# Four graph-attention layers in one kernel: who orders the instructions of layers 1 to 3

## The chip, the cores and the metric

The kernel runs on one core of a Trainium2 chip. The metric is the device time of one execution in microseconds (us). A core has five engines that work side by side, each through its own queue in order: TensorE (PE: matrix products; PEld is its weight load), VectorE (DVE), ScalarE (ACT), GpSimd (POOL) and SyncE (SP, which issues transfers). Transfers run on 16 DMA engines. TensorE reads from SBUF and writes its products to PSUM[...].

## What is computed

The input is `x` (4096 rows of 256 numbers) and an adjacency matrix `adj` (4096 x 4096, int32), which has many more edges among the first nodes than among the last. Four attention layers follow each other. Each is added to its input and normalised:

```python
x = _layernorm(x + L0(x, positions, curv_feats, adj, ...))   # 8 heads, with a curvature term
x = _layernorm(x + L1(x, adj, ...))                          # 1 head
x = _layernorm(x + L2(x, adj, ...))                          # 4 heads, elu, residual, its own layer norm
x = _layernorm(x + L3(x, adj, ...))                          # three attention passes, elu after each
```

One pass of layer 3 stands for the kind of work:

```python
Wh = h @ W
e = jax.nn.leaky_relu(Wh @ a[:F] + (Wh @ a[F:]).T, ALPHA)
att = jax.nn.softmax(jnp.where(adj > 0, e, NEG_INF), axis=1)
h = jax.nn.elu(att @ Wh)
```

Layer 1's scores depend on the source node alone within a row's softmax, so its weights are the mask itself times a factor of the source node. Layer 2 does the same as layer 3 for four heads of 64 columns.

## The kernel before

Layer 0 runs first, takes 1379 us of the profiled execution, and writes lists of the nodes that matter to each group of rows. The change doesn't touch it. Layers 1, 2 and 3 (three passes) have one frame, `attend` (L1240).

**Tiles.** The 4096 rows are cut into 16 pairs of row tiles (2 x 128 = 256 rows, `PW`). For one pair, the sum over the source nodes runs over tiles of 128 nodes. The first pairs take all 32 tiles ("dense": 6 pairs in layer 1, 1 in layer 2, 3 in layer 3) and read the values from SBUF (`Vp` or `V`). For the other pairs only listed nodes count, 13 to 25 tiles a pair, and their rows are gathered by GpSimd into `g` (L1284, 1010 gathers in all). `sequence` mixes both kinds into one list of (pair, tile).

**One step of the list.** `weights` makes the weights `w` of a tile from the mask (loaded by SP, L1278):
- layer 1: a cast of the mask, on ACT and DVE in turn (L1382), and for listed tiles a split of `g` in two parts, on ACT (L1359) and then DVE (L1360);
- layer 2: four instructions on DVE, one a head (L1474);
- layer 3: one instruction on DVE (L1567).

`products` multiplies the weights of earlier steps: layer 1 into `acc` (L1393), layer 3 into `acc` (L1573), two row tiles each. Layer 2 takes two tiles at a time (`batch=2`): first the eight products `num` (L1483, 64 columns each, heads in turn in the lower and upper half of the columns), then the eight products `den` (L1487, one column each, four places). A matrix product of this type stands as two records in the trace, in layer 1 as one.

**The ending of a pair.** When a pair's last tile is multiplied, the generator `one` divides, normalises and projects its two row tiles for the next layer. Its instructions hop between engines. In layer 3, for each row tile: `inverse` on DVE (L316 to L318), `y` on ACT (L1583), `y` on DVE (L1585), `elu_neg` twice on ACT (L307, L308), `y` on DVE (L310); then either transposes on TensorE (`xT_p`, L196), copies on ACT (L198) and the projection `ph` (L207), or, in the third pass, the residual (L1589), moments (L301, L302) and the layer norm (L333 to L339). In layer 2, `num` and `den` are copied to `sb` on ACT (L1497, L1498), transposed on TensorE into `pt` (L1505), divided (L316 to L318, L1510), and go through elu and two layer norms before the transposes of `xT_p`.

**The order.** `attend` walks the list and takes a few steps of the ending after each tile (`rate` steps, one `yield` each). So the ending of an earlier pair is interleaved with the weights and products of later ones. This interleaving is written into the source, and `tc.manual_schedule` holds PE, DVE and ACT to the order of the source:

```python
with tc.manual_schedule(engines={mybir.EngineType.PE, mybir.EngineType.DVE, mybir.EngineType.Activation}):
    ...
    for q, k, A, listed in seq:
        if k == 0:
            states[q] = opened(q, A, listed)
        ready.append((states[q], k, weights(states[q], k), k == A - 1))
        if len(ready) == lag + batch:
            multiply(batch)
        due += rate
        while due >= 1.0:
            due -= 1.0
            next(end, None)
```

Outside such a block, the tile scheduler orders the instructions when the kernel is built. It runs through the program with its own estimate of each instruction's duration, and gives an engine that comes free the earliest instruction of the source that it takes to be ready. SP and POOL are ordered so in the whole kernel, and so is everything outside `attend`.

**Buffers.** There are six buffers for `w` in each layer (a buffer of layer 2 holds four heads), six for the masks (four tiles each), 16 for `g` in layers 1 and 2 and 20 in layer 3. In PSUM, six `acc` serve three pairs; layer 2 has three `num` and three `den`. Two more banks serve all other products.

**The seams.** A layer starts when the last row of its projection is there: sums (L229 to L237), extremes (`spread_p`, `spread_q`, L252 to L260), in layers 2 and 3 a row factor that is written to memory and read back as `R` (L290 and on), and the scaling of `V`.

Of the kernel before, what the change touches and what calls it, by code (L numbers as in the profile page):

```python
# [78 lines left out]
def gnn_stack(ctx: ExitStack, tc: tile.TileContext, a: dict, out: bass.AP):  # L79
# [37 lines left out]
    def drain(steps):  # L117
        for _ in steps:
            pass
# [1120 lines left out]
    def attend(seq, opened, weights, products, ends, rate=1.0, batch=1, lag=2):  # L1240

        states, ready, ended, due = {}, [], [], 0.0
        end = ends(ended)
        with tc.manual_schedule(engines={mybir.EngineType.PE, mybir.EngineType.DVE, mybir.EngineType.Activation}):
            def multiply(n):
                some, ready[:] = ready[:n], ready[n:]
                products(some)
                ended.extend(state for state, _, _, last in some if last)  # L1250
# [11 lines that stand above are left out]
            while ready:  # L1262
                multiply(min(batch, len(ready)))
            drain(end)
# [78 lines left out]
    def layer1(proj, nxt, seq):  # L1343
        with ExitStack() as st:
# [51 lines left out]
            def one(state, n):  # L1396
# [14 lines left out]
                yield from project(nxt, ys, q * PW)  # L1411

            attend(seq, opened, weights, products, lambda ended: ends_of(ended, NP, nxt, ps, one))
            nxt.sums()

# [5 lines left out]
    def layer2(proj, V, nxt, seq):  # L1421
# [3 lines left out]
        with ExitStack() as st:  # L1425
# [64 lines left out]
            def one(state, n):  # L1490
# [35 lines left out]
                yield from project(nxt, ys, q * PW)  # L1526

            attend(seq, opened, weights, products, lambda ended: ends_of(ended, NP, nxt, ps, one), rate=1.6, batch=2)
            nxt.sums()

    def layer3(n, proj, V, nxt, seq):
        s = 1.0 - 0.01
        with ExitStack() as st:
# [41 lines left out]
            def one(state, m):  # L1575
# [18 lines left out]
                else:  # L1594
                    yield from project(nxt, ys, q * PW)

            attend(seq, opened, weights, products, lambda ended: ends_of(ended, NP, nxt, ps, one))
            if nxt is not None:
                nxt.sums()
# [110 lines left out]
```

## Time and profile before

| | |
|---|---|
| median of 3 runs | 3496.66 us (3496.36 to 3497.55) |
| the profiled execution's own time | 3482.08 us |
| its span | 3480.4 us |
| TensorE busy | 2684.1 us, 77% of the span |
| VectorE busy | 2300.2 us, 66% |
| GpSimd busy | 1941.0 us, 56% |
| ScalarE busy | 1349.4 us, 39% |
| mean granted TensorE clock | 0.824 |

The median and the profiled execution are different executions, 14.6 us apart. All durations of single instructions come from the profiled one. A line of the groups of instructions names source line, engine, operation, output and inputs, and count; "idle before" is time in which the engine stood still until the named instruction, on its own or another engine, let it go on. Matmuls are pipelined and their ends are modelled, so consecutive records overlap; what one costs in a row of them is read from the distance between starts. A busy share is a mean over stages that have different limits, so the span is cut into stages below.

### The profile page before, as it was taken

Reading aid. Unit: us, or ns where it says so; the run is one execution under the profiler, and the core shown is the slowest. Engines: PE = TensorE matmul, PEld = TensorE weight load, DVE = VectorE, ACT = ScalarE, POOL = GpSimd, SP = SyncE. Lnnn points to the kernel's source line nnn. Section 1 sums busy time; section 2 is a strip of 40 time slices with the busy share of each in tenths; the row PEclk is TensorE's granted clock in tenths of the full one; section 3 lists DMA queues with packets and bytes.
Section 4 is the critical chain, followed back from the end, with each engine's and each line's share of the span. In section 5 each row is a group of like instructions: output and inputs, shape, how many; then the busy total and the mean of one; then the engine's idle time right before and its main releaser. Section 6 shows DMA issues by size and latency. Waiting matters only on the chain. (4 is left out here: it accounts for less than half of the span.)

```text
span 3480.4 us, 53129 instructions
## 1 busy us (share of the span) xinstructions
PE 2684.1 (77%) x15814; PEld 1998.9 (57%) x15814; DVE 2300.2 (66%) x7414; ACT 1349.4 (39%) x3868; POOL 1941.0 (56%) x1874
## 2 busy tenths in 40 slices
PE   6475567767778766888688787777699989989885
PEld 5354455555556554777544333333488868867674
DVE  7798877786555443555488888778455545545665
ACT  3354446554445443455431222233312222232333
POOL 0264555666777761455158655553177637746772
PEclk8576656667787666988899999999799989989998
DMA  6587777664444443555343333332444454436552
GB/s 183 160 263 247 223 224 234 192 204 117 119 121 115 122 112 113 172 147 144 99 125 101 100 99 100 97 90 57 130 135 137 118 156 135 136 95 185 154 154 81
DMA packets 345903, 495.62 MB, mean 142 GB/s; under 512 B 120444, under 2 KB 252386, under 8 KB 345602
## 3 DMA queue, kind: packets, MB, share of 16 engines
q0 software_dynamic: 87600, 252.16, 25.9%
q1 hardware_dynamic: 239576, 223.18, 21.6%
q10 hardware_dynamic: 18432, 16.79, 1.4%
q8 instruction: 131, 2.15, 0.3%
q14 instruction: 164, 1.34, 0.1%
HBM read 426.20 MB, written 65.72 MB: 141 GB/s over the span
## 5 line engine op out<-in xcount | busy, mean ns | idle before, releaser
L1284 POOL DMA_INDIRECT g<-table,pair_idx x1010 | 1111.5, 1101 | 597.9 <-PE den L1487 95.8
L648 POOL DMA_INDIRECT g<-table,idx x445 | 502.1, 1128 | 285.2 <-issue 151.3
L1573 PE MATMUL acc<-g,w 128*128 128x257 f32 x2448 | 576.7, 384 | 36.3 <-DVE w L1567 36.3
L1573 PEld LDWEIGHTS acc<-g,w 128*128 128x128 f32 x2448 | 461.1, 191 | 112.6 <-DVE w L1567 49.0
L1474 DVE SCALAR_TENSOR_TENSOR w<-R,g,mask 128x256 f32<-128x256 f32 x1004 | 425.4, 493 | 23.0 <-PE den L1487 18.5
L1483 PE MATMUL num<-w,g 128*64 128x256 f32 x2008 | 319.5, 422 | 51.6 <-DVE w L1474 50.9
L1567 DVE SCALAR_TENSOR_TENSOR w<-R,g,mask 128x256 f32<-128x256 f32 x612 | 282.1, 480 | 100.4 <-PE acc L1573 98.0
L1003 POOL DMA_INDIRECT pair_m<-in_adjT,cell x251 | 269.7, 1075 | 136.7 <-issue 46.0
L692 PE MATMUL acc<-g,to_row 128*128 128x264 f32 x890 | 325.9, 528 | 18.3 <-DVE g L679 16.2
L1573 PE MATMUL acc<-V,w 128*128 128x257 f32 x1152 | 288.3, 390 | 22.4 <-DMA R<-r_d 17.5
L692 PEld LDWEIGHTS acc<-g,to_row 128*128 128x128 f32 x890 | 225.9, 268 | 77.6 <-DVE g L679 20.5
L1483 PEld LDWEIGHTS num<-w,g 128*64 128x64 f32 x2008 | 157.5, 148 | 196.1 <-DVE w L1474 135.0
L1573 PEld LDWEIGHTS acc<-V,w 128*128 128x128 f32 x1152 | 221.4, 195 | 60.2 <-ACT V L1553 18.1
L1583 ACT ACTIVATE y<-acc,inverse 128x256 f32<-128x256 f32 x96 | 45.6, 475 | 516.2 <-DVE inverse L318 444.2
L207 PE MATMUL ph<-wx,xT 128*128 128x258 f32 (+3 forms) x640 | 204.4, 456 | 34.7 <-ACT xT L198 30.0
L628 PE MATMUL x<-what,of_row 128*128 128x40 f32 (+4 forms) x890 | 157.1, 350 | 55.9 <-DVE of_row L625 54.3
L891 DVE FIND_INDEX8 cand<-ones,near 128x8 uint16<-128x520 bf16 (+8 forms) x424 | 195.0, 469 | 0.0
L628 PEld LDWEIGHTS x<-what,of_row 128*128 128x128 f32 x890 | 153.2, 265 | 66.4 <-DVE of_row L625 54.9
L686 ACT ACTIVATE to_row<-count,side 128x128 f32<-128x128 f32 x445 | 145.3, 391 | 115.1 <-PE acc L692 111.4
L1007 DVE TENSOR_SCALAR pair_mb<-pair_m 128x256 uint8<-128x256 int32 x251 | 74.8, 300 | 172.0 <-DMA pair_m<-in_adjT,cell 153.5
L1567 DVE SCALAR_TENSOR_TENSOR w<-R,V,mask 128x256 f32<-128x256 f32 x288 | 135.3, 480 | 69.9 <-PE acc L1573 55.1
L207 PEld LDWEIGHTS ph<-wx,xT 128*128 128x128 f32 x640 | 137.0, 224 | 73.9 <-ACT xT L198 44.8
(325 smaller groups left out, 4608.1 us busy)
## 6 DMA issues: line engine op xcount, KB each, us to landing
ai<-in_adj SPq DMA_DIRECT2D x124, 512.0 KB
mask<-listed_d SPq DMA_DIRECT2D x228, 128.0 KB
at<-in_adjT SPq DMA_DIRECT2D x96, 256.0 KB
mask<-mask_d SPq DMA_DIRECT2D x128, 128.0 KB
g<-table,pair_idx POOLq DMA_INDIRECT x1010
R<-r_d SPq DMA_DIRECT2D x56, 256.0 KB
table<-V POOLq DMA_DIRECT2D x12, 1032.0 KB
s<-y ACTq DMA_DIRECT2D x96, 128.0 KB
```

The lines of the kernel that those rows point to most:

```text
L207: nc.tensor.matmul(ph, xT[:, kt, :], self.wx[:, kt, :], start=kt == 0, stop=kt == 1 and self.bias is None)
L628: nc.tensor.matmul(self.x[:, t], of_row[:, t], ls.what, start=True, stop=True)
L648: nc.gpsimd.indirect_dma_start(self.g[:, t, :], None, table0[:, :], bass.IndirectOffsetOnAxis(ap=self.idx[:, t:t + 1], axis=0))
L686: nc.scalar.activation(self.to_row[:, t], count, AF.Abs, bias=self.side[:, t, 0:1])
L692: nc.tensor.matmul(acc, self.to_row[:, t], self.g[:, t, 0:VW], start=self.t0 + t == 0, stop=last and t == n - 1)
L891: nc.vector.max_index(cand[:, s], ones8, near[:, at:at + W])
L1003: nc.gpsimd.indirect_dma_start(m[:, :], None, pair_cells, bass.IndirectOffsetOnAxis(ap=cell[:, k:k + 1], axis=0))
L1284: nc.gpsimd.indirect_dma_start(g[:, :], None, self.table[:, :], bass.IndirectOffsetOnAxis(ap=pair_idx[:, at:at + 1], axis=0))
L1474: nc.vector.scalar_tensor_tensor(w[:, h], R[:, h].rearrange("p t i -> p (t i)"), g[:, VW2 + h:VW2 + h + 1], m, ALU.max, ALU.mult)
L1483: nc.tensor.matmul(num[h % 2 * D2:(h % 2 + 1) * D2, h // 2, :], g[:, h * (D2 + 1):h * (D2 + 1) + D2], w[:, h], start=False, stop=last and ...
L1567: nc.vector.scalar_tensor_tensor(w, R[:, q * PW:(q + 1) * PW], g[:, C + 1:C + 2], m, ALU.max, ALU.mult)
L1573: nc.tensor.matmul(t, w[:, it * P:(it + 1) * P], g[:, 0:C + 1], start=k == 0, stop=last)
```

## The change

In `attend`, the block that holds PE, DVE and ACT to the order of the source becomes an ordinary block. These engines are then ordered by the tile scheduler in layers 1 to 3 too. The source still sets the order in which the scheduler prefers instructions. Nothing else in the source differs.

```diff
         states, ready, ended, due = {}, [], [], 0.0
         end = ends(ended)
-        with tc.manual_schedule(engines={mybir.EngineType.PE, mybir.EngineType.DVE, mybir.EngineType.Activation}):
+        if True:
             def multiply(n):
                 some, ready[:] = ready[:n], ready[n:]
                 products(some)
```

## The prediction

> **What bounds the kernel now.** I read the page's engine shares first (TensorE 77%, VectorE 66%, no engine full), so the answer differs by stage. I then cut the span where the lines of a layer begin and end, and asked for busy times per stretch. Columns: stretch, length, busy us (instructions) of PE, PEld, DVE, ACT and POOL, granted TensorE clock, DMA share, GB/s.
>
> ```profile
> 1420.00:1699.00 279.00, 240.36 (x1470) 216.32 (x1469) 155.72 (x532) 145.03 (x499) 139.17 (x143) 0.89 0.49 140
> 1699.00:1741.00 42.00, 17.23 (x57) 11.52 (x55) 13.74 (x56) 16.69 (x65) 1.41 (x2) 0.73 0.31 96
> 1741.00:2453.00 712.00, 565.00 (x4844) 266.64 (x4844) 589.05 (x1557) 204.07 (x617) 392.17 (x285) 0.91 0.34 94
> 2453.00:2488.00 35.00, 7.71 (x29) 4.78 (x25) 11.40 (x48) 18.92 (x52) 0.96 (x1) 0.64 0.26 77
> 2488.00:2783.00 295.00, 294.24 (x1376) 255.94 (x1376) 170.76 (x448) 73.85 (x274) 204.71 (x207) 0.99 0.51 143
> 2783.00:2811.00 28.00, 11.28 (x32) 6.94 (x32) 7.96 (x37) 14.77 (x52) 0.94 (x1) 0.63 0.25 78
> 3136.00:3456.00 320.00, 276.43 (x1193) 227.08 (x1192) 198.69 (x552) 98.14 (x166) 202.96 (x206) 0.97 0.54 151
> ```
>
> In order: layer 1, the seam to layer 2, layer 2, its seam, layer 3's first pass and its seam, layer 3's third pass. The second pass and its seam (2811 to 3136) look like the first. Layer 0, 1379 us, is not touched. The first pass is TensorE's, with 0.8 us idle of 295. The third has 183 fewer instructions and takes 25 us longer. In layer 2 neither TensorE nor VectorE is full: VectorE, the busier, stands idle 123 us.
>
> The waits say why. Columns: waiting instruction, what ended the wait, us in total, times, longest. The first three lines are layer 2, the others layer 3's third pass.
>
> ```profile
> PE xT_p L196 <- ACT y L339: 84.1, 15, 6.5
> ...
> PE num L1483 <- DVE w L1474: 50.9, 50, 3.1
> DVE inverse L316 <- PE pt L1505: 50.6, 14, 7.1
> ...
> PE acc L1573 <- DVE w L1567: 41.2, 24, 2.5
> ...
> DVE inverse L316 <- PE acc L1573: 33.9, 14, 2.6
> DVE y L310 <- ACT elu_neg L308: 33.8, 29, 2.2
> ```
>
> These are blocked queues: an instruction of a row tile's ending stands at the head and waits, with ready products or weights behind it. In the third pass VectorE waits 67.7 us on `acc` and `elu_neg`, then TensorE lacks `w` for 41.2 us.
>
> The last view is TensorE's timeline in layer 2. Columns: start, time until the last ends, instruction; a product of one head is two records.
>
> ```profile
> 2049.72 1.95 PE L1483 MATMUL num<-w,g 128*64 128x256 f32 x16
> 2051.59 1.04 PE L1487 MATMUL den<-w,g 128*1 128x256 f32 x16
> 2052.57 0.55 PE L1505 MATMUL pt<-ident,sb 128*128 128x128 f32 x3
> ...
> 2450.53 1.04 PE L1487 MATMUL den<-w,g 128*1 128x256 f32 x16
> 2451.51 1.08 PE L1483 MATMUL num<-w,g 128*64 128x256 f32 x8
> 2452.52 0.61 PE L1487 MATMUL den<-w,g 128*1 128x256 f32 x8
> ```
>
> From start to the next start, 8 `num` cost 1.87 us, 4 `num` 1.01, 8 `den` 0.98. So two `num` (different heads) take (1.87 - 1.01) / 2 = 0.43 us together and each run of `num` 1.87 - 4 x 0.43 = 0.15 more. A run of `den`, with four heads sharing 0.43 us, costs 0.98 - 2 x 0.43 = 0.12 more. **The order of products is a cost of its own here.**
>
> **What the Trainium skill says.** "TensorEngine Tiling (Array Packing)", Key Properties: different tiles of the array run in parallel, and "Changing tiling mode (not just tile) drains the TensorE". The trace agrees: 64-column `num` pair, one-column `den` go in fours, and a change costs 0.12 to 0.15 us. "TensorE: Matmul & The Clock Gate", Architectural detail: ScalarE and VectorE are strict FIFO; Part 2 says that matmuls stay in program order. The waits above are what that means. The same page, Part 1: idle TensorE is throttled. Here the clock is 0.63 to 0.73 in the seams and 0.99 in the first pass.
>
> **The change part by part.** No instruction, transfer or buffer size is added or removed: only the `with` goes, so the tile scheduler puts the instructions of PE, DVE and ACT where its own times say that they are ready. I compared the instruction orders of both programs; the counts are from there. The order of SP's and POOL's issues shifts by places too, but POOL is busy 392 of 712 us in layer 2 and its gathers have 16 buffers and more; I cost that at nothing. If the cover went, 251 gathers in layer 2 late by 0.3 us each would be 75 us.
>
> *Layer 3's third pass.* Before, VectorE meets `inverse` 2 weights after a tile's last one; after, 5 (six buffers hold them). The two row tiles of a pair run their endings side by side with weights between, so the 2.2 us wait for `elu_neg` (a table load on ACT) has four weights in front. At most 7 instructions stand between two weights, some 2.8 us (six of 0.43, one of 0.18), against 5 weights x 0.86 us of products (four records at 294.24 / 1376 = 0.214 us) = 4.3 us in stock. TensorE at the first pass's rate needs 1193 x 0.214 = 255 us instead of 320: 65 at most. VectorE's own work is 199, but some waits will stay; I take **-45** (-20 to -65).
>
> *First and second pass.* TensorE is full, and the order of its products and transposes is the same before and after: **0**. The cover is TensorE itself; if a transpose is late by 1 us per row tile, 64 us are lost, my upper end.
>
> *Layer 1.* TensorE idles 279 - 240 = 39 us, on the weights, `Vg` and transposes; the transposes now stand 45 to 66 products after the tile's end instead of 26 to 64. I take three quarters, **-30** (-10 to -50, the lower end with some clock won).
>
> *Seams.* In the source's order the last row tiles end one after the other. At 1699 two pairs take 14 and 13 us in turn; after, they overlap: -12. Layer 2's seam has one pair, two tiles: -4. The first and second pass end with two pairs of 10 us in turn: -8 each. The tail from 3456 to 3480 is the same chain: -10. Together **-42** (-20 to -55). What comes next at each seam, the projection's sums and the load of `R`, is not shortened.
>
> *Layer 2.* VectorE is unblocked: its waits for `pt` (50.6), `den` (18.5) and `elu_neg` (16.2) can go, and 589 us of work stays. But where TensorE was short of `w`, the scheduler took `den` of a head as soon as its `num` was in. The runs go from 142 + 142 (141 of 8 each) to 487 of `num` (227 of one) and 452 of `den` (259 of one). Pairs of `num` go from 566 to 696, fours of `den` from 283 to 517. Price before: 566 x 0.43 + 142 x 0.15 + 283 x 0.43 + 142 x 0.12 = 404 us. After: 696 x 0.43 + 487 x 0.15 + 517 x 0.43 + 452 x 0.12 = 649. Transposes and projections take some 55 us more (16 pairs x 3.4). So TensorE needs 459 before and **704 after**, over VectorE's 589 and about the 712 that the stage takes now. The 84.1 us wait for `y` before the transposes goes (they stand some 33 heads behind the `pt` instead of 24), but TensorE is now the bound: **0** (-50 if a lone head overlaps its neighbour somewhat, +60 if waits for `w` add to the full TensorE).
>
> Sum: -45 + 0 - 30 - 42 + 0 = -117. The profiled execution took 3482.08 us (span 3480.4 and 1.7 around it), so 3365; the median is 14.6 us above it, so **3380** on its scale.
>
> **The rivals.**
> *A, as above*: 0.55, 3380.
> *B, layer 2 gains too*: VectorE's bound, 589 us plus some waits, holds because lone `num` and `den` overlap. For it: before, VectorE was the busier. Against it: no `num` overlaps a `den` in the trace. Layer 2 at 642 would give 3380 - 70 = 3310. 0.15.
> *C, new waits for old*: the scheduler's times differ from the chip's, half of the 117 comes, and layer 2 loses 40: 3497 - 58 + 40 = 3479. For it: an order fixed by wrong times blocks the same FIFO queues. Against it: in layer 3 the counts above leave slack. 0.15.
> *D, slower*: the hand-over between `num` and `den` is dearer for a lone head than in long runs[...]. TensorE then runs layer 2 well over 704. It decides when the 117 us are lost there: over 939 runs, 0.125 us more each, that is 0.25 to 0.28 instead of 0.12 to 0.15. At 0.2 more, +188 - 117 gives 3568. For it: single runs never occur before, so the price is carried over from runs of 4 and 8. Against it: every change of mode in the trace costs about the same. 0.12, and 0.03 for a result within 0.2%.
> That the change does nothing is out: the orders differ on all three engines.
>
> **How the numbers follow.** The likeliest, A, gives 3380. The range takes A's bounds, most of B and of C: 3300 to 3480. Faster by over 0.2% (about what a measurement of this kernel can tell from no change, 7 us): A, B and C, 0.85. Same 0.03, slower 0.12.
>
> **What would show it.** Layer 3's third pass at about 275 us with TensorE over 90% busy and the waits for `w` nearly gone; passes one and two still 295 to 297; each seam shorter by 8 to 12 us; in layer 2 short runs of `num` and `den` in turn, a lone head costing 0.43 + 0.15 + 0.43 + 0.12 = 1.13 us, TensorE the busier engine, and VectorE waiting for `den`. Layer 2 under 660 makes B right. Layer 2 over 800, with over 0.25 us lost at each change, makes D right. A first pass over 310, or a third pass still over 305, means that the new order blocks too.

## The result, and the profile after

The changed kernel takes 3335.27 us (median of 4 runs, 3333.80 to 3349.82) beside 3497.11 us of the kernel before (4 runs): a ratio of 0.9546 with a 95% interval of 0.9519 to 0.9573, 162 us less. The profiled execution has a span of 3332.1 us and a mean granted clock of 0.855 (0.824 before).

First, the same cut by stage as in the prediction. This is the table of busy times per stretch of the kernel after; columns: stretch, length, busy us (instructions) of PE, PEld, DVE, ACT and POOL, granted TensorE clock, DMA share, GB/s.

```profile
1430.00:1633.00 203.00, 201.26 (x1448) 189.61 (x1447) 143.51 (x529) 146.43 (x500) 144.20 (x145) 1.00 0.68 193
1633.00:1665.00 32.00, 19.76 (x72) 13.33 (x70) 12.91 (x60) 16.70 (x67) 1.41 (x2) 0.78 0.42 129
1665.00:2369.00 704.00, 703.55 (x4820) 249.85 (x4824) 566.60 (x1553) 200.76 (x616) 389.57 (x285) 1.00 0.34 95
2400.00:2694.00 294.00, 292.89 (x1367) 255.05 (x1368) 174.73 (x449) 71.98 (x275) 206.09 (x207) 0.99 0.51 143
2694.00:2713.00 19.00, 9.26 (x43) 6.11 (x41) 7.30 (x35) 13.42 (x51) 0.94 (x1) 0.89 0.36 108
3027.00:3317.00 290.00, 271.08 (x1200) 224.66 (x1200) 190.93 (x558) 94.80 (x172) 204.31 (x207) 1.00 0.59 169
```

In order: layer 1 without its first part, the seam to layer 2, layer 2, layer 3's first pass and its seam, layer 3's third pass. Layer 1 now keeps TensorE busy throughout at full clock (before: 240 of 279 us at 0.89). In layer 2 TensorE is busy in 703.55 of 704 us. Layer 2's clock, 0.91 before, is 1.00. The seams are shorter and run at a higher clock, and the third pass still leaves TensorE 19 us without work.

The exact lengths, from the first to the last attention product of each layer in the two traces (a seam is the time between two of them, the tail the time behind the last; the predicted column repeats the steps of the prediction):

| stage | before, us | after, us | difference | predicted |
|---|---|---|---|---|
| up to layer 1's first product | 1378.8 | 1391.3 | +12.5 | 0 |
| layer 1 | 321.1 | 242.0 | -79.1 | -30 |
| seam to layer 2 | 42.0 | 32.1 | -9.9 | -12 |
| layer 2 | 711.2 | 704.0 | -7.2 | 0 |
| seam to layer 3 | 35.4 | 31.2 | -4.2 | -4 |
| layer 3, first pass | 294.2 | 293.9 | -0.3 | 0 |
| seam | 28.1 | 18.4 | -9.7 | -8 |
| second pass | 293.5 | 294.6 | +1.1 | 0 |
| seam | 28.2 | 19.3 | -8.9 | -8 |
| third pass | 321.1 | 289.8 | -31.3 | -45 |
| tail | 26.6 | 15.4 | -11.2 | -10 |

The rows add up to -148, the difference of the two spans. The first row is no effect of an order that changed: layer 0 is the same, and over the traces of comparable runs its length lies anywhere from 1379 to 1405 us. Without it the stages bring 161 us. The third pass is at its shortest in this trace: in five other comparable traces with the same layer 3 it takes 292.7 to 293.6 us, so its gain is 28 to 31 us.

Second, what VectorE and TensorE wait for after the change. Columns: waiting instruction, what ended the wait, us in total, times, longest. The first three lines are layer 2 (VectorE, then TensorE), the last three the third pass.

```profile
DVE inverse L316 <- PE pt L1505: 73.1, 19, 8.8
DVE w L1474 <- PE den L1487: 52.3, 36, 3.2
...
PE num L1483 <- ACT V L1455: 2.5, 1, 2.5
...
DVE w L1567 <- DMA g<-table,pair_idx: 58.4, 73, 2.4
DVE w L1567 <- PE acc L1573: 35.8, 83, 1.2
...
PE acc L1573 <- DVE w L1567: 18.4, 22, 1.4
```

In layer 2 the direction has turned round: before, TensorE waited 84.1 us for `y` and 50.9 us for `w`; now VectorE waits for `pt` and `den`, and TensorE for 2.5 us. In the third pass the waits for `inverse` and `elu_neg` (33.9 and 33.8 us before) are gone from the top. In their place VectorE waits 58.4 us for the gathers `g`, which it had not waited for in the lines of before.

Third, TensorE's timeline in layer 2 after the change. Columns: start, time until the last ends, instruction, records (two a head).

```profile
1694.46 0.65 PE L1483 MATMUL num<-w,V 128*64 128x256 f32 x4
1695.04 0.59 PE L1487 MATMUL den<-w,V 128*1 128x256 f32 x2
1695.57 0.65 PE L1483 MATMUL num<-w,V 128*64 128x256 f32 x4
1696.15 0.60 PE L1487 MATMUL den<-w,V 128*1 128x256 f32 x6
```

These are the short runs. Two heads of `num` cost 0.58 us from start to next start (0.43 + 0.15 in the prediction), one head of `den` 0.53 (0.43 + 0.12).

### The profile page after: what moved, and what is told of

Same layout as the page of the kernel before. It is cut to its first block, busy times and chain, and to the rows that moved or that the text cites. A ratio compares the mean times of both kernels' runs of the same rounds, so it can differ in the third digit from the quotient of the medians.

```text
span 3332.1 us, 53082 instructions
## 1 busy us (share of the span) xinstructions
PE 2771.2 (83%) x15814; PEld 1953.9 (59%) x15814; DVE 2262.0 (68%) x7414; ACT 1333.9 (40%) x3866; POOL 1947.7 (58%) x1874
## 4 chain that ended last, share of the span: by engine, by line
PE 48%; DMA 4%; DVE 3%; ACT 2%; issue 1%; POOL 0%; SPq 0%; ACTq 0%; DVEq 0%; POOLq 0%
PE acc L1573 19%; PE num L1483 11%; PE den L1487 8%; PE acc L1393 4%; PE ph L207 4%; DMA g<-table,pair_idx 3%; PE xT_p L196 1%; PE pr L213 1%; DVE w L1567 1%; PE pt L1505 0%; POOL g L1284 0%; ACT V L1553 0%; DMA V<-V_d 0%; DMA table<-V 0%; DVE y L1585 0%
## 5 line engine op out<-in xcount | busy, mean ns | idle before, releaser
L1474 DVE SCALAR_TENSOR_TENSOR w<-R,g,mask 128x256 f32<-128x256 f32 x1004 | 440.9, 491 | 48.0 <-PE den L1487 47.9
L1567 DVE SCALAR_TENSOR_TENSOR w<-R,g,mask 128x256 f32<-128x256 f32 x612 | 292.0, 482 | 244.2 <-PE acc L1573 165.0
L1483 PE MATMUL num<-w,g 128*64 128x256 f32 x2008 | 367.6, 395 | 0.0
L1003 POOL DMA_INDIRECT pair_m<-in_adjT,cell x251 | 276.8, 1103 | 133.3 <-issue 44.2
L692 PE MATMUL acc<-g,to_row 128*128 128x264 f32 x890 | 326.6, 529 | 20.5 <-DVE g L679 18.4
L1487 PE MATMUL den<-w,g 128*1 128x256 f32 x2008 | 266.5, 378 | 0.0
L1483 PEld LDWEIGHTS num<-w,g 128*64 128x64 f32 x2008 | 140.5, 135 | 196.9 <-DVE w L1474 95.2
L207 PE MATMUL ph<-wx,xT 128*128 128x258 f32 (+3 forms) x640 | 183.7, 420 | 23.6 <-ACT xT L198 19.3
```

The costliest lines, as they stand in the source:

```text
L207: nc.tensor.matmul(ph, xT[:, kt, :], self.wx[:, kt, :], start=kt == 0, stop=kt == 1 and self.bias is None)
L692: nc.tensor.matmul(acc, self.to_row[:, t], self.g[:, t, 0:VW], start=self.t0 + t == 0, stop=last and t == n - 1)
L1003: nc.gpsimd.indirect_dma_start(m[:, :], None, pair_cells, bass.IndirectOffsetOnAxis(ap=cell[:, k:k + 1], axis=0))
L1474: nc.vector.scalar_tensor_tensor(w[:, h], R[:, h].rearrange("p t i -> p (t i)"), g[:, VW2 + h:VW2 + h + 1], m, ALU.max, ALU.mult)
L1483: nc.tensor.matmul(num[h % 2 * D2:(h % 2 + 1) * D2, h // 2, :], g[:, h * (D2 + 1):h * (D2 + 1) + D2], w[:, h], start=False, stop=last and ...
L1487: nc.tensor.matmul(den[32 * h:32 * h + 1, :], g[:, (h + 1) * (D2 + 1) - 1:(h + 1) * (D2 + 1)], w[:, h], start=False, stop=last)
```

## The experiments

**1. Which layer brings what.** `attend` got an argument `hold`; the layer named holds TensorE, VectorE and ScalarE to the source's order again, the other two stay with the scheduler.

```diff
-    def attend(seq, opened, weights, products, ends, rate=1.0, batch=1, lag=2):
+    def attend(seq, opened, weights, products, ends, rate=1.0, batch=1, lag=2, hold=()):
...
-        if True:
+        with tc.manual_schedule(engines=set(hold)) if hold else nullcontext():
...
-            attend(seq, opened, weights, products, lambda ended: ends_of(ended, NP, nxt, ps, one))
+            attend(seq, opened, weights, products, lambda ended: ends_of(ended, NP, nxt, ps, one), hold=(PE, DVE, ACT))
```

Layer 1 held. 

> The source's order of TensorE, VectorE and ScalarE held again in layer 1 alone; layers 2 and 3 stay with the scheduler. Theory (each layer's gain is its own: layer 1 and the seam behind it fell from 321.1 + 42.0 to 242.0 + 32.1 us): layer 1 back at about 320 us with the granted clock at 0.89 again, the other stages as in the changed kernel, the whole 3335 + 79 + 10 = about 3420 (3405 to 3430). Rival (layer 1's shorter time came from its start or from what layer 0 hands over, not from its own order): layer 1 stays near 242 and the whole near 3340.

Layer 2 held. 

> The source's order held in layer 2 alone: the runs of num and den are 142 + 142 again instead of 487 + 452. Theory (in layer 2 the freed queues are paid back by the short runs on TensorE): layer 2 at about 711 instead of 704, its seam 35 instead of 31, the whole 3335 + 11 = about 3346 (3335 to 3357). Rival (layer 2's own new order brought a real gain that the stage lengths hide): over 3370. Rival (the short runs cost more than the freed queues bring): under 3325.

Layer 3 held. 

> The source's order held in layer 3 alone, all three passes. Theory: third pass at 321 instead of 290 us, first and second pass unchanged at 294, seams 28 instead of 19 us, tail 27 instead of 15: 31 + 9.7 + 8.9 + 11.2 = 61 more, the whole about 3396 (3385 to 3407). Rival (the third pass gained from the state that layers 1 and 2 leave, such as the clock): less than 40 more.

| held | median, us | ratio to before (95%) | stages that moved against the kernel after |
|---|---|---|---|
| layer 1 | 3429.97 | 0.9804 (0.9778 to 0.983) | layer 1 324.5 (+82.5), its seam 42.0 (+9.9) |
| layer 2 | 3354.55 | 0.9595 (0.9569 to 0.962) | layer 2 710.2 (+6.2), its seam 35.9 (+4.7) |
| layer 3 | 3394.80 | 0.9704 (0.9684 to 0.9725) | third pass 322.9 (+33.1), seams 28.0 and 28.2 (+9.6, +8.9), tail 25.0 (+9.6) |

The stage differences are 92 + 11 + 61 = 164 us, close to the 161 of the whole: the gains of the three layers add up, and each layer's gain lies in its own order. All three theories held, layer 1's at the upper end of its range; their rivals (layer 1 from its start, a gain or a loss hidden in layer 2, a third pass helped by earlier layers) are out. Half of the whole change is layer 1 itself, for which the prediction had a quarter.

**2. Why layer 1 gained twice its idle time.** The granted clock shows most of it. In each of these traces the clock is either 0.50 or 1.00, and all its changes lie on one grid of 3.41 us. This is the table of five such windows around one stall, in the kernel with layer 1 held.

```profile
1594.96:1598.38 3.42, 3.42 (x31) 3.42 (x30) 2.94 (x10) 1.79 (x6) 2.65 (x3) 1.00 0.66 186
1598.38:1601.79 3.41, 0.95 (x8) 0.68 (x7) 3.17 (x13) 0.55 (x3) 2.65 (x3) 1.00 0.61 148
1601.79:1605.20 3.41, 3.41 (x15) 3.28 (x15) 1.03 (x5) 2.61 (x10) 2.31 (x3) 0.50 0.71 202
1605.20:1608.61 3.41, 3.41 (x20) 2.96 (x20) 1.39 (x4) 1.75 (x9) 1.50 (x2) 1.00 0.57 165
1608.61:1612.03 3.42, 3.42 (x25) 3.22 (x24) 1.82 (x7) 2.28 (x8) 1.18 (x2) 1.00 0.31 97
```

TensorE's timeline of the same kernel names the stall, and shows the products before and after it:

```profile
1597.47 1.12 PE L1394 MATMUL acc<-Vg,w 128*128 128x258 f32 x8
1598.43 0.64 PE L1394 MATMUL acc<-Vp,w 128*128 128x258 f32 x4
1601.53 1.26 PE L1394 MATMUL acc<-Vg,w 128*128 128x258 f32 x4 [2.46 <-ACT rs L333]
1602.59 1.06 PE L1394 MATMUL acc<-Vp,w 128*128 128x258 f32 x4
1603.45 0.63 PE L196 MATMUL xT_p<-ident,y 128*128 128x128 f32 x2
```

Eight products take 0.96 us from start to start before the stall, 0.12 each. The stall of 2.46 us leaves TensorE 0.95 us of work in its window (0.28). The window behind it runs at 0.50, and four products take 0.86 us and more, 0.22 each; the next has 1.00 again. So this stall is paid twice: once as idle time, once in the products behind it.

Whether a stall is paid twice depends on how much of a window it empties. Over layer 1 in the five kernels of the table below, 41 windows at full clock had TensorE busy, as the profile models it, for less than half: 39 of them were followed by half clock. Of 44 windows busy for 0.5 to 0.7, 13 were; of 269 busy for more than 0.7, none. Half clock ended behind each of 52 windows that were busy for 0.9 or more, and went on behind each of 17 that were busy for less than 0.8.

To see which queue makes the stalls, the source's order of layer 1 was held on one side only: `hold=(PE,)` in one kernel, `hold=(DVE, ACT)` in the other.

> In layer 1 the source's order is held on TensorE alone; VectorE and ScalarE are left to the scheduler. With all three held layer 1 took 324.5 us, with none 242 to 245. Theory (the queue that blocks is VectorE's: with all held it stands 68.9 us at `res` for `pr` and 45.1 us at `Vg` for ScalarE's half, while TensorE's own waits name weights and table tiles): layer 1 at 245 to 270. Rival (TensorE's order is the one that blocks, its transposes and projections stand where their inputs are late): layer 1 at 290 or more.

> In layer 1 the source's order is held on VectorE and ScalarE; TensorE is left to the scheduler. Theory (VectorE's queue blocks): layer 1 at 300 to 325, clock at 0.90 or less. Rival (TensorE's order blocks): layer 1 at 245 to 270 and the clock near 1.00.

The first runs of the two fell on a chip on which the kernel before took 3894 us and layer 0 alone some 150 us more, so only the kernels of that batch can be compared with each other: layer 1 at 365.5 us (TensorE held) and 373.8 (VectorE and ScalarE held), where two others of the batch with a free layer 1 had 326.5 and 336.7. Both were run again:

> The same kernel as m1_pe, for a layer 1 beside 242 (free) and 324.5 us (all three held). In the last batch both halves took 365 and 374 us where the free order took 321 to 337, so neither queue alone is free. Theory now (a stall of either queue idles TensorE and halves its clock for the products behind it, so each order held alone costs a part): 260 to 300 us. Rival (one order carries all of it): within 8 us of 243 or of 324.

> The same kernel as m1_dve. Theory now (each order held alone costs a part): 260 to 310 us, above m1_pe_again as in the last batch. Rival (one order carries all of it): within 8 us of 243 or of 324.

Layer 1 took 295.5 us with TensorE held and 312.0 (expected: 260 to 310) with VectorE and ScalarE held, one run each. The first theory (VectorE's queue alone) and its rival (TensorE's alone) both fall: each order costs by itself, 54 and 70 us beside the 242.0 of the kernel after, and together they cost 82 and not the sum. The waits of TensorE show where. With TensorE alone held (first fence) it waits 29.8 us for the `y` of its transposes, beside 1.1 us in the kernel before (third fence): that ScalarE, now free, brings `y` later than the old place of the transposes expects is the likely reason, not shown. With the others held (second fence), it waits for weights and the halves of `Vg`, as before.

```profile
PE xT_p L196 <- ACT y L339: 29.8, 11, 5.7
PE acc L1394 <- ACT Vp L1360: 10.4, 4, 3.3
```

```profile
PE acc L1394 <- DVE w L1383: 17.5, 15, 2.0
PE acc L1394 <- DVE Vg L1361: 10.3, 7, 1.7
PE acc L1394 <- ACT Vg L1360: 8.7, 8, 1.8
```

```profile
PE acc L1393 <- DVE w L1382: 14.6, 14, 2.3
PE acc L1393 <- DVE Vg L1360: 11.0, 7, 1.7
PE acc L1393 <- ACT Vp L1359: 7.2, 3, 3.3
PE ph L207 <- ACT xT L198: 6.8, 10, 1.2
...
PE xT_p L196 <- ACT y L339: 1.1, 3, 0.4
```

The five kernels together give the price. A stall is counted where two starts of TensorE lie over 0.6 us apart; idle and busy are those of the whole layer, and the last column is the part of the busy time that lies in windows of half clock.

| layer 1 | stalls | idle, us | TensorE busy, us | of it at half clock, us |
|---|---|---|---|---|
| after (all free) | 8 | 9 | 233 | 12 |
| TensorE held | 28 | 45 | 251 | 41 |
| VectorE and ScalarE held | 41 | 50 | 262 | 58 |
| before | 47 | 49 | 272 | 67 |
| all held | 49 | 50 | 275 | 73 |

The same products need 18, 29, 39 and 42 us more than after. As an estimate, work at 0.50 lasts twice as long (0.22 beside 0.12 us a product, above, is nearly that), so the clock costs half of the added time at half clock: 14, 23, 27 and 31 us, some three quarters. The other 4 to 12 us stay open; the busy time is modelled and can take in short waits. The busy time doesn't follow the idle time: 45 us of idle in 28 stalls cost 18 us of it, 50 us in 49 stalls 42.

**3. What bounds layer 2.** The `den` products of a batch may only be issued behind its last `num`; all engines stay free otherwise. The runs of `num` fall from 487 to 185, those of `den` from 452 to 163.

```diff
-                        nc.tensor.matmul(num[h % 2 * D2:(h % 2 + 1) * D2, h // 2, :], g[:, h * (D2 + 1):h * (D2 + 1) + D2], w[:, h],
+                        after = nc.tensor.matmul(num[h % 2 * D2:(h % 2 + 1) * D2, h // 2, :], g[:, h * (D2 + 1):h * (D2 + 1) + D2], w[:, h],
...
-                for (_, _, _, den, _), k, (g, w), last in some:
-                    for h in range(H2):
-                        nc.tensor.matmul(den[32 * h:32 * h + 1, :], g[:, (h + 1) * (D2 + 1) - 1:(h + 1) * (D2 + 1)], w[:, h],
+                with tc.issue_after(after.ins):
+                    for (_, _, _, den, _), k, (g, w), last in some:
+                        for h in range(H2):
+                            nc.tensor.matmul(den[32 * h:32 * h + 1, :], g[:, (h + 1) * (D2 + 1) - 1:(h + 1) * (D2 + 1)], w[:, h],
```

> As the changed kernel, but in layer 2 the den products of a batch of two heads' tiles may only be issued behind the batch's last num product; VectorE and ScalarE stay free. The runs of num fall from 487 to 185, so pairs and fours are shared again. Theory (layer 2 is bound by TensorE, 704 us of work, of which the short runs are the larger part): TensorE needs about 590 x 0.43 + 185 x 0.15 + 283 x 0.43 + 145 x 0.12 + 55 = 476 us, VectorE with 567 us of its own work becomes the busier, and layer 2 takes 600 to 650: the whole 3335 - 54 to - 104, about 3255 (3230 to 3285). Rival (the run price does not matter, since TensorE would only idle more and VectorE's waits for pt and den set layer 2): 3335 within 10. Rival (queueing den behind num delays the endings and blocks VectorE as before): 3340 or more.

It takes 3241.52 us, a ratio of 0.9255 (0.9228 to 0.9283): 94 us less than the kernel after. Layer 2 falls from 704.0 to 601.1 us, and no other stage moves by more than 4 us. Its table of stretches, and then what VectorE and TensorE wait for there:

```profile
1669.00:2270.00 601.00, 567.10 (x4824) 256.01 (x4824) 557.17 (x1552) 200.31 (x613) 449.46 (x285) 1.00 0.40 111
```

```profile
PE num L1484 <- DVE w L1475: 27.1, 37, 2.1
...
DVE w L1475 <- DMA g<-table,pair_idx: 16.9, 5, 4.9
DVE inverse L316 <- PE pt L1507: 13.7, 12, 2.1
```

TensorE waits for `w` again and VectorE is busy in 557 of 601 us: the bound has gone from TensorE to VectorE. TensorE's 567 us are more than the 476 worked out, but its ends are modelled and take in waits inside a run: of the 110 runs of eight `num` the shortest is 1.88 us from start to next start, the mean 2.65. The `den` runs, which need no new weights, sum to 150 us (268 us in the kernel after). That is what the prediction's prices give for the 163 runs with 304 fours of this trace; the 139 worked out ahead took 145 runs with 283. The rivals, by which layer 2 would stay at 704 or slow down, are out.

**4. What bounds the third pass.** The number of pairs that read whole tiles from SBUF there is 3; it was made 2 and 4.

```diff
-                layer3(n, p, V, nxt[0], plan(3))
+                layer3(n, p, V, nxt[0], plan(3) if n < 3 or not sparse else sequence(range(2), range(2, NP), LEAD[3]))
```

> As the changed kernel, but in the third pass of layer 3 the pairs of row tiles that read whole table tiles are 2 instead of 3; the pair that changes sides has some 22 more gathers on GpSimd and some 3 tiles' products fewer. Theory (the third pass is now bound by the gathers, 1.05 us and 0.3 between two): 22 x 1.35 = 30 us longer, third pass about 320. Rival (TensorE bounds it): 3 x 0.86 = 2.6 us shorter, about 288 to 291.

> The other way: 4 such pairs instead of 3, some 20 gathers fewer and 3 tiles' products more. Theory (gather-bound): the gathers fall to 184 x 1.35 = 248 us plus a start of some 14, TensorE needs 271 + 2.6 = 274 and takes over, third pass 276 to 284 instead of 290 to 293. Rival (TensorE-bound): 292 to 296.

These two were in the batch on the slower chip; within it the third pass took 371.6 us with 2 pairs, 346.2 and 346.6 with 3 (the kernels of experiment 2), 323.3 with 4. The side with more gathers was run again:

> The same kernel as den2, beside best4 on one chip, since the last batch's times (before: 3894 us) are not comparable with the others. Theory (gather-bound): third pass about 320 us. Rival (TensorE-bound): 288 to 291.

The third pass took 318.2 us, 28.4 more than in the kernel after (25 more than in the five other traces named above), with 22 more gathers and fewer products: the gathers bound it, and the rival falls. VectorE's wait for them grew, as the waits of this kernel show:

```profile
DVE w L1568 <- DMA g<-table,pair_idx: 90.7, 118, 2.4
DVE w L1568 <- PE acc L1574: 30.2, 67, 1.2
```

GpSimd's timeline names the two ends of the chain. Columns: start, us, instruction, idle before it and releaser. In the kernel after, the first and the last gather of the third pass are:

```profile
3048.73 1.12 POOL L1284 DMA_INDIRECT g<-table,pair_idx  x1 [13.94 <-PE acc L1573]
...
3311.11 1.09 POOL L1284 DMA_INDIRECT g<-table,pair_idx  x1 [0.30 <-issue]
```

In the kernel before they are:

```profile
3154.41 1.04 POOL L1284 DMA_INDIRECT g<-table,pair_idx  x1 [13.88 <-DMA mask<-listed_d]
...
3427.02 0.95 POOL L1284 DMA_INDIRECT g<-table,pair_idx  x1 [0.31 <-DVE bn_st L301]
```

After, the first gather starts 21.8 us behind the first product (the table that it reads must be written), 203 steps of 1.29 us follow, and the last product ends 5.6 us behind the last gather's start: 289.8 us. Before, the first gather starts just as late, and the last stands 26.7 us ahead of the end; between them the step was 1.34 us, since twelve gathers started more than 0.5 us behind the end of the one ahead. That was the slack of this pass, and the change used it up.

**5. Both together.** The kernel of experiment 3 with 4 pairs in the third pass:

> The kernel grp (den behind the batch's last num in layer 2) with 4 instead of 3 pairs of whole table tiles in layer 3's third pass. Theory (gathers bound the third pass at 204 x 1.35 us): third pass 276 to 284 us instead of 293.5 in grp, the rest as in grp, the whole 3241.5 - 13 = about 3228. Rival (TensorE bounds the third pass): 2.6 us longer, about 3244.

It takes 3217.04 us, a ratio of 0.9188 (0.9168 to 0.9208), the fastest of all, 118 us below the kernel after. The third pass takes 272.4 us instead of 293.5, more gained than the expected 276 to 284. The stretch of this pass and VectorE's waits in it:

```profile
2934.00:3206.00 272.00, 272.00 (x1248) 237.93 (x1248) 198.17 (x571) 95.14 (x173) 186.62 (x187) 0.99 0.62 173
```

```profile
DVE w L1569 <- PE acc L1575: 60.9, 158, 1.2
...
DVE w L1569 <- DMA g<-table,pair_idx: 1.5, 4, 0.4
```

VectorE's wait for gathers has fallen from 58.4 to 1.5 us, and TensorE is busy throughout. It does more products than in the kernel after (1248 records beside 1200) in about the 271 us that these took there; the 18.4 us that TensorE spent waiting for weights are gone.

## Why the prediction was right, point by point, and where it was not

The forecast was 3380 us (-117), within 3300 to 3480; measured is 3335 (-162). The mechanism of rival A held: blocked queues, freed. Two terms of its sum were mis-sized, by 49 us and, the other way, by 14. That the second offsets a part of the first is luck.

**Layer 1 (-30, measured -79): mis-sized.** The idle part came out 10 us larger than the 30: TensorE's idle time fell from 49 to 9 us over the whole layer, 40 us. The reason given, that the transposes stand later, covers the smaller part: of the waits before, transposes and their projections had 8 us (1.1 and 6.8), weights and the halves of the values some 36. What failed above all is the clock, which the step took in with "the lower end with some clock won": TensorE's busy time for the same products fell from 272 to 233 us, 39 more, of which the clock accounts for some 27, by the estimate of experiment 2. The 0.89 stood in the first line of the table shown in the prediction, beside 0.99 for a pass without idle time. 240 us of work at 0.89 are 214 at 1.00, so 26 us more could have been taken from that line alone, and the upper bound of -50 was too near.

The prediction had cited the Trainium skill, "TensorE: Matmul & The Clock Gate", Part 1, for the throttle of an idle TensorE, and applied it to the seams only. That part names an idle window of about 3.4 us as what brings the slow state. Here a window of 3.41 us with 2.46 us of idle was enough for 0.50 in the next, and 39 of 41 windows that were less than half busy did the same: the window need not be idle throughout, and a layer that is 85% busy can still lose a tenth of its speed. Its "Busy/warm" state, reached after one busy window of about that length, agrees: the clock was 1.00 again 3.41 us later.

**Third pass (-45, measured -31): mis-sized.** Its reasoning on VectorE held: the waits for `elu_neg` fell from 33.8 to 1.9 us. But it gave 275 us with the waits for `w` nearly gone, and of 41.2 us of them 18.4 are left. The step that failed is the sentence that costs GpSimd's queue at nothing. It argued from layer 2, where gathers take 392 of 712 us, and never asked for the third pass, whose line said 202.96 us busy of 320. With the 0.30 us between two gathers, which the busy time leaves out, 204 of them fill 262 us behind a start of 22 us. This floor, 284 us and the last products, could be read from the trace of before.

**Layer 2 (0, measured -7): right, term by term.** TensorE was to need 704 us and the stage takes 704.0. The starts in the trace give 374 us for the runs of `num` (696 x 0.43 + 487 x 0.15 = 372), 268 for `den` (517 x 0.43 + 452 x 0.12 = 276) and 62 for the rest (55). Its prices were read where the clock was 1.00, while the layer ran at 0.91 before; that it would be 1.00 after was taken for granted, and came true. A lone head of `num` costs 0.58 us and of `den` 0.52, so a change costs no more in short runs than in long ones: rival D, which needed 0.125 us more at each, is out. VectorE's bound of rival B does exist, at about 600 us, but only once the runs are long again (experiment 3).

**Seams and tail (-42, measured -44)** and **passes one and two (0, measured -0.3 and +1.1): right**, each seam within 3 us of its number. The endings of several tiles now run side by side: at the end of layer 3's first pass the last four `inverse` start within 4 us (13 us before), and layer 3 held brings the old 28 us back. Rival C, half of the gains and a loss of 40 us in layer 2, did not come.

## What to carry to other kernels

An idle time of TensorE can cost twice, by its length and by slow products behind it. In these traces the second cost came behind windows of 3.41 us that were less than about half busy, so the same idle time cost more where it was spread over more windows; read the granted clock of the stage beside its idle time. Before a stall is counted as gain, find the floor of each other queue in that very stage, from its first start to its last and with the gaps between its instructions, since busy shares leave these out. And where a scheduler is given the order, look at what it can't know: short runs of products, which change kind more often and leave heads without a partner to share a step with, cost 94 us here, and one constraint, `den` behind the batch's last `num`, won them with everything else left free.

## What was not expected of the hardware

The granted TensorE clock fell to 0.50 for the next window of 3.41 us behind nearly every window of layer 1 that was less than half busy (39 of 41), and behind none of 269 that were more than 0.7 busy. A change between 64-column and one-column products costs the same 0.12 to 0.15 us whether the run is of one head or of eight: the Trainium skill, "TensorEngine Tiling (Array Packing)", Key Properties, says that a change of tiling mode drains TensorE, without a price; that the two kinds differ in tiling mode is inferred from their column counts. Gathers of 128 rows kept a step of 1.25 us (0.95 busy, 0.30 between), 1.29 in the mean of the third pass.
